# Second feed-forward products in Strassen's form, norms moved to the scalar engine, and a new order of the steps, in a two-layer graph network

## Chip, cores, metric

One core of one Trainium2 chip. The metric is the device time of one execution in microseconds (us); I quote the median of the runs of a kernel with the lowest and the highest. All runs compared here were in the fast state. Engine names are those of the profile: PE is the matrix engine (TensorE), PEld its weight loads, DVE the vector engine (VectorE), ACT the scalar engine (ScalarE), POOL GpSimd. `L338` is line 338 of the kernel whose profile is shown, so line numbers differ by kernel.

## The reference, cut to what matters

The input is `x`, 128 graphs of 128 nodes and 256 features in f32, with an adjacency matrix for each. Two layers follow. Each ends in a feed-forward network of 256 → 1024 → 256 with residual and layer norm.

```python
# layer 0: attention in 8 heads, values chosen by relation r
scores = einsum('bhid,bhjd->bhij', q, k) / sqrt(dh);  attn = softmax(scores)
out = sum over r of einsum('bhij,bhjd->bhid', attn * (adj == r), v_r)
x = ln(src + out @ Wo + bo, g1, beta1)                     # norm 0
x = ln(x + gelu(x @ W1 + b1) @ W2 + b2, g2, beta2)         # norm 1
# layer 1: two graph attentions, then
h = ln(x + gat(gat(x)), g_ln1, b_ln1)                      # norm 2
return ln(h + relu(h @ w_ff1 + b_ff1) @ w_ff2 + b_ff2)     # norm 3
```

## The kernel before

It works in 32 groups of four graphs (T = 512 rows). Every phase of a group is a Python generator, and `in_order(...)` takes steps from several generators in a list written by hand. The instructions then run in that order on each engine. In the loop the first feed-forward network (`f1`) and the graph layer (`l1`) of one group, the second network (`f2`) of another, and projections (`pr`) and attention (`at`) of a third lie between one another. The first product of each network is already in Strassen's form (7 products in place of 8); the second is plain. `seeded` is one PSUM bank into which products are added on top of a copied start.

```python
def added(S, i, p, po, res):               # residual sum into a new tile, statistics
    ...
    nc.vector.tensor_add(flat(t[:, pair(p), :]), po, flat(res[:, pair(p), :]))
    for s in range(2):
        nc.vector.bn_stats(...); nc.vector.bn_aggr(...)

def normed(S, i, bs=slice(0, G)):          # (x - mean) * rs, on VectorE
    for b in range(bs.start, bs.stop):
        nc.vector.tensor_scalar(t[:, b, :], t[:, b, :], mv[:, b, 0:1], rs[:, b : b + 1],
                                op0=ALU.subtract, op1=ALU.mult)

# in ffn(), after the first product:       # the plain second product
for p in range(G // 2):
    po = ps_1.tile([P, T], F32, tag="fe" if p else "fa", ...)
    for s in range(2):
        b = 2 * p + s
        for f in range(NF):
            nc.tensor.matmul(po[:, s * D : (s + 1) * D], hT[:, f, b * P : (b + 1) * P],
                             wb_[:, f, :], start=(f == 0), stop=(f == NF - 1))
            ...
    added(S, i, p, po, S["res", i - 1])

# the end of the program
in_order((f2, 14), (n2, 2), (n3, 4), lambda: store(S), (f2, 4))
checks()
```

Of the kernel before, what the change touches and what calls it, by code (L numbers as in the profile page):

```python
# [24 lines left out]
G = 4  # L25
# [4 lines left out]
class Weights:  # L30
# [41 lines left out]
    def constants(self):  # L72
        nc = self.nc
        self.ident = self.tile([P, P], "ident")
        make_identity(nc, self.ident)
        self.ones = self.tile([P, P // 4], "ones")
        nc.vector.memset(self.ones, 1.0)
        self.eps = self.tile([P, 1], "eps")
        nc.vector.memset(self.eps, EPS)
        self.mhalf = self.tile([P, G], "mhalf")  # L80
        nc.vector.memset(self.mhalf, -0.5)
# [22 lines left out]
def fast_pass(ctx, tc, a, out):  # L104
# [17 lines left out]
    io = ctx.enter_context(tc.tile_pool(name="io", bufs=2))  # L122
# [3 lines left out]
    small = ctx.enter_context(tc.tile_pool(name="small", bufs=4))  # L126
    dram = ctx.enter_context(tc.tile_pool(name="dram", bufs=2, space=bass.MemoryType.DRAM))
# [4 lines left out]
    def load_xT(g):  # L132
        xt = w1p.tile([P, NCH, T], F32, tag="xT", name=f"xT_{g}")
        nc.sync.dma_start(
            xt, xT[:, g * T : (g + 1) * T].rearrange("(c p) t -> p c t", p=P)
        )
        return xt
# [9 lines left out]


    k.constants()
    first = {"g": 0}  # L150
    first["xt"] = load_xT(0)
# [9 lines left out]
    first["ad"], first["xr"] = load_rest(0)  # L161
# [19 lines left out]
    FH = FF // 2  # L181
    B11, B21, B22, T4, T1, T2, T3 = range(7)

    def forms(name):

        w = k.tile([P, 7, FH], "w_" + name)
        for i, c, h in ((B11, 0, 0), (B21, 1, 0), (B22, 1, 1), (T1, 0, 1)):
            nc.sync.dma_start(
                w[:, i], a[name][c * P : (c + 1) * P, h * FH : (h + 1) * FH]
            )  # L190
        return w

    def combined(w):
        for o, p, q in ((T3, B22, T1), (T1, T1, B11), (T2, B22, T1), (T4, B21, T2)):
            nc.vector.tensor_sub(w[:, o], w[:, p], w[:, q])
# [9 lines left out]
    w2 = k.w("L0_gnn_W2")  # L205
# [3 lines left out]
    u2 = k.w("L1_gnn_w_ff2")  # L209
# [57 lines left out]
    def transposed(y, gc, bc, n):  # L267

        yT = w3p.tile([P, NCH, T], F32, tag="yT", name="yT_" + n)
# [14 lines left out]
    def added(S, i, p, po, res):  # L284

        n = f"{i}_{S['g']}"
        if p == 0:
            S["t", i] = w3p.tile([P, G, D], F32, tag="t", name="t_" + n)
            S["mv", i] = (
                c_out[:, S["g"]] if i == 3  # L290
                else small.tile([P, G, 2], F32, tag="mv", name="mv_" + n)
            )
        t, mv = S["t", i], S["mv", i]
        nc.vector.tensor_add(flat(t[:, pair(p), :]), po, flat(res[:, pair(p), :]))
        st = small.tile([P, 2, 6], F32, tag="st", name=f"st_{n}_{p}")
        for s in range(2):
            nc.vector.bn_stats(st[:, s, :], t[:, 2 * p + s, :])  # L297
            nc.vector.bn_aggr(mv[:, 2 * p + s, :], st[:, s, :])
# [8 lines left out]
    def normed(S, i, bs=slice(0, G)):  # L307

        t, mv, rs = S["t", i], S["mv", i], S["rs", i]
        for b in range(bs.start, bs.stop):  # L310
            nc.vector.tensor_scalar(  # L311
                t[:, b, :], t[:, b, :], mv[:, b, 0:1], rs[:, b : b + 1],
                op0=ALU.subtract, op1=ALU.mult,
            )
# [5 lines left out]
    def scaled(S, i, p):  # L320
        t = S["t", i]
        if p == 0:
            S["res", i] = t if i == 3 else w3p.tile(
                [P, G, D], F32, tag="res", name=f"res_{i}_{S['g']}"
            )
        o = S["res", i]
        nc.vector.tensor_mul(o[:, pair(p)], t[:, pair(p)], over(rows[i][0], 2))
        nc.vector.tensor_add(o[:, pair(p)], o[:, pair(p)], over(rows[i][1], 2))

    def norm(S, i):  # L330
# [5 lines left out]
        for p in range(G // 2):  # L336
            scaled(S, i, p)
# [4 lines left out]
    def turned(S, i):  # L342
        n = f"{i}_{S['g']}"
        S["xT", i + 1] = yT = transposed(S["t", i], *cols[i], n)
# [7 lines left out]
        nc.vector.tensor_sub(ys[:, 1], ys[:, 0], a11)  # L352
        nc.vector.tensor_sub(ys[:, 3], a12, ys[:, 1])

    def ffn(S, i, wa, ba, func, wb_):

        n = f"{i}_{S['g']}"
        yT, ys = S["xT", i], S["yS", i]
        a11, _, a12, a22 = (yT[:, c, h * TH : (h + 1) * TH] for c in range(2) for h in range(2))
        s1, s2, s3, s4 = (ys[:, m] for m in range(4))  # L360
        hT = w1p.tile([P, NF, T], F32, tag="hT", name="hT_" + n)
        RN = NF // 4

        def product(bank, form, m, r, start=False):


            for s in range(2):
                f = 2 * r + s
                nc.tensor.matmul(  # L369
                    bank[:, s * TH : (s + 1) * TH], wa[:, form, f * P : (f + 1) * P], m,  # L370
# [3 lines left out]
        def hidden(r, k2, h):  # L374

            f = k2 * NF // 2 + 2 * r
            return hT[:, f : f + 2, h * TH : (h + 1) * TH]

        def activated(src, r, k2, h):
            for s in range(2):  # L380
                f = k2 * NF // 2 + 2 * r + s
                nc.scalar.activation(  # L382
                    hidden(r, k2, h)[:, s], src[:, s * TH : (s + 1) * TH] if src is not None
                    else hidden(r, k2, h)[:, s], func, bias=ba[:, f : f + 1],
# [13 lines left out]
        for r in range(RN):  # L398
            pe = ps_1.tile([P, T], F32, tag="fe", name=f"ph7_{n}_{r}")
# [5 lines left out]
            u2 = w1p.tile([P, T], F32, tag="u2", name=f"u2_{n}_{r}")  # L405
            nc.scalar.copy(u2, seeded)
# [3 lines left out]
            yield  # L410
            product(pe, T4, a22, r)
            nc.vector.tensor_add(hidden(r, 0, 1), halves(pe), halves(u2))  # L412
            activated(None, r, 0, 1)
            yield
            product(seeded, T1, s1, r)
            nc.vector.tensor_add(hidden(r, 1, 1), halves(seeded), halves(p7))  # L416
            activated(None, r, 1, 1)
# [5 lines left out]
            activated(seeded, r, 1, 0)  # L423
            if r + 1 < RN:
                nc.scalar.copy(seeded, pa)
            yield
        for p in range(G // 2):
            po = ps_1.tile([P, T], F32, tag="fe" if p else "fa", name=f"po_{n}_{p}")
            for s in range(2):
                b = 2 * p + s  # L430
                for f in range(NF):
                    nc.tensor.matmul(  # L432
                        po[:, s * D : (s + 1) * D], hT[:, f, b * P : (b + 1) * P], wb_[:, f, :],
                        start=(f == 0), stop=(f == NF - 1),
                    )
                    if f == NF // 2 - 1 or (f == NF - 1 and s == 0):
                        yield
            added(S, i, p, po, S["res", i - 1])
            yield
# [4 lines left out]
    def second_ffn(S):  # L444
        yield from ffn(S, 3, u1, c1, AF.Relu, u2)

# [11 lines left out]
    def entered(g):  # L458

        xt = load_xT(g)  # L460
        ad, xr = load_rest(g)
        return dict(xt=xt, ad=ad, xr=xr, g=g)

    def prepared(S):
        g, xr, ad = S["g"], S["xr"], S["ad"]
# [64 lines left out]
    def sums(S, p):  # L530

        e, pm = S["e", p], S["pm", p]
# [21 lines left out]
        den = rd.rearrange("p u c i -> p (u c i)")  # L554
# [3 lines left out]
        nc.vector.tensor_reduce(c_att[:, 0, g, p : p + 1], den, AX.X, ALU.min)  # L558
        nc.vector.reciprocal(den, den)  # L559
        for u in range(2):  # L560
            bs = slice((2 * p + u) * P, (2 * p + u + 1) * P)
            nc.vector.tensor_mul(oT[:, :, bs], pav[:, u], rd[:, u])

    def attention(S):
# [3 lines left out]
        for p in range(G // 2):  # L568
# [4 lines left out]
            sums(S, p)  # L573
            yield
        for p in range(G // 2):
# [8 lines left out]
            added(S, 0, p, po, S["xr"])  # L584
            yield

    def spread(columns, n):
# [3 lines left out]
        line = small.tile([G, P], F32, tag="line", name="line_" + n)  # L591
# [7 lines left out]
    def edges(target, source, S, l):  # L599
# [3 lines left out]
        for b in range(G):  # L603
            nc.scalar.activation(  # L604
                s[:, b, :], target[:, b, :], AF.Identity, bias=source[:, b, :]
            )
        nc.vector.scalar_tensor_tensor(s, s, ALPHA, s, op0=ALU.mult, op1=ALU.max)
        yield
        nc.scalar.activation(s, s, AF.Exp)
# [12 lines left out]
    def layer1(S):  # L622
# [28 lines left out]
        for p in range(G // 2):  # L651
# [7 lines left out]
            added(S, 2, p, po, S["res", 1])  # L659
        yield  # L660

    def store(S, bs=slice(0, G)):
# [3 lines left out]
            S["t", 3][:, bs],  # L666
# [436 lines left out]
```

## Time and profile before

| | before |
|---|---|
| time, median of 4 runs | 2887.47 us (2886.09 to 2888.1) |
| TensorE / weight loads / VectorE / ScalarE busy | 98% / 76% / 70% / 45% |
| TensorE's streaming, counted | 2751.5 us |
| span less streaming ("lost") | 136.6 us |
| of it: first 60 us / between / last 108 us | 27.3 / 74.3 / 34.9 us |

Streaming is not a view of the profile. I multiply each TensorE record by the start-to-start pace of its kind in stretches without a wait, as the prediction does below (its sum with rounded paces is 2749; the full count gives 2751.5). The rest of the span is "lost": waits, and time at a lower clock. It is needed because the busy share hides waits of a few hundred ns, as the modelled ends reach over them. The same counting is used for all kernels below.

One more view of before is wanted for later: the timeline of TensorE in its last 90 us, four of the lines with a wait. The columns are start, length, engine, line, operation, count; in brackets the idle time ahead and what ended it.

```profile
2820.79 3.81 PE L643 MATMUL py<-wh,gs 128*128 128x258 f32 x8 [3.86 <-DVE gs L619]
2836.68 1.99 PE L655 MATMUL pg<-yh,gs 128*128 128x256 f32 x8 [0.83 <-DVE gs L619]
2843.88 2.30 PE L273 MATMUL pt<-ident,t 128*128 128x128 f32 x8 [3.48 <-DVE t L311]
2881.21 0.19 PE L769 MATMUL pflag<-ones,good 128*1 128x1 f32 x2 [4.84 <-DVE good L767]
```

Near the end no other group is left to fill in, so each hand-over to VectorE is open. After the wait of 3.86 us eight matmuls took 3.81 us, twice their usual time: the clock had been lowered.

### The profile page before, as it was taken

How to read it: one execution, taken by the hardware profiler on the slowest of the kernel's cores; microseconds unless marked ns; L12 is line 12 of the kernel's file. 1: busy time of each engine (PE TensorE's matmuls, PEld its weight loads, DVE VectorE, ACT ScalarE, POOL GpSimd, SP SyncE). 2: the span in 40 equal slices, each digit the busy share in tenths (PEclk: the TensorE clock that was granted, in tenths of full speed). 3: DMA queues.
4: the chain of work that ended last, by engine and by line, in shares of the span. 5: the costliest groups of instructions: out<-in, count | busy, mean ns of one | idle time of the engine just before them, and what ended most of it. 6: DMA issues, size and time to landing. Idle time of an engine off the chain costs nothing.

```text
span 2888.1 us, 44301 instructions
## 1 busy us (share of the span) xinstructions
PE 2839.6 (98%) x17744; PEld 2206.1 (76%) x17744; DVE 2015.8 (70%) x4595; ACT 1312.5 (45%) x2759; POOL 141.5 (5%) x137
## 2 busy tenths in 40 slices
PE   7999999999999999999999999999999999999997
PEld 4677777777787777787777777777877777877775
DVE  6577666777667777667776677776677776677764
ACT  3435445445455345454454454453553444544542
POOL 0000000000000000000000000000000000000000
PEclk9999999999999999999999999999999999999998
DMA  5000111010111000110001110101110001101000
GB/s 152 23 27 12 34 34 34 23 34 12 34 34 34 23 26 20 34 34 26 30 12 34 34 34 23 34 12 34 34 33 24 20 26 34 34 26 30 12 19 20
DMA packets 68469, 86.82 MB, mean 30 GB/s; under 512 B 8096, under 2 KB 46368, under 8 KB 68256
## 3 DMA queue, kind: packets, MB, share of 16 engines
q1 hardware_dynamic: 67424, 83.52, 9.2%
q8 instruction: 141, 2.31, 0.3%
q14 instruction: 72, 0.59, 0.1%
q10 hardware_dynamic: 832, 0.40, 0.0%
HBM read 66.99 MB, written 16.91 MB: 29 GB/s over the span
## 4 chain that ended last, share of the span: by engine, by line
PE 95%; DVE 2%; ACT 1%; DMA 1%; SPq 0%; issue 0%; POOL 0%; ACTq 0%; DVEq 0%; POOLq 0%
PE po L432 30%; PE ph L369 15%; PE seeded L369 12%; PE pq L483 7%; PE pv L493 7%; PE pw L630 4%; PE pwo L580 4%; PE pav L546 4%; PE pt L273 3%; PE ps L511 2%; PE pden L537 2%; PE py L643 2%; PE pg L655 2%; ACT hT L382 0%; DVE rd L559 0%; DVE st L297 0%
## 5 line engine op out<-in xcount | busy, mean ns | idle before, releaser
L432 PE MATMUL po<-w_L_gnn_W,hT 128*128 128x256 f32 x2048 | 480.7, 383 | 0.0
L432 PE MATMUL po<-w_L_gnn_w_ff,hT 128*128 128x256 f32 x2048 | 463.3, 380 | 0.0
L432 PEld LDWEIGHTS po<-w_L_gnn_W,hT 128*128 128x128 f32 x2048 | 384.8, 190 | 87.5 <-issue 37.0
L432 PEld LDWEIGHTS po<-w_L_gnn_w_ff,hT 128*128 128x128 f32 x2048 | 385.1, 190 | 54.2
L305 POOL TENSOR_TENSOR rs<-rs,mhalf 128x4 f32<-128x4 f32 x129 | 138.9, 1076 | 2702.5 <-DVE rs L304 2702.5
L517 ACT ACTIVATE e<-ps 128x512 f32<-128x512 f32 x256 | 132.3, 603 | 295.8 <-PE ps L511 295.8
L493 PE MATMUL pv<-wv,xT 128*128 128x512 f32 x512 | 240.7, 593 | 2.0 <-ACT e L517 2.0
L297 DVE BATCH_NORM_STATS2 st<-t 128x6 f32<-128x256 f32 x512 | 210.4, 411 | 8.8
L559 DVE RECIPROCAL rd<-rd 128x512 f32<-128x512 f32 x64 | 214.6, 3353 | 2.2
L412 DVE TENSOR_TENSOR hT<-ph,u 128x512 f32<-128x512 f32 x128 | 88.1, 688 | 178.7 <-ACT hT L382 128.6
L369 PE MATMUL seeded<-yS,w_L_gnn_w_ff 128*128 128x256 f32 x768 | 204.3, 388 | 4.2 <-DVE hT L416 2.8
L369 PE MATMUL seeded<-yS,w_L_gnn_W 128*128 128x256 f32 x768 | 199.7, 382 | 1.5 <-DVE hT L416 0.8
L311 DVE TENSOR_SCALAR t<-t,mv,rs 128x256 f32<-128x256 f32 x384 | 132.5, 408 | 92.5 <-POOL rs L305 92.5
L369 PEld LDWEIGHTS seeded<-yS,w_L_gnn_W 128*128 128x128 f32 x768 | 143.1, 190 | 66.6 <-issue 37.1
L369 PE MATMUL ph<-yT,w_L_gnn_W 128*128 128x256 f32 x768 | 193.1, 381 | 0.4 <-ACT yT L276 0.4
L369 PE MATMUL ph<-yT,w_L_gnn_w_ff 128*128 128x256 f32 x768 | 191.1, 385 | 0.0
L396 ACT COPY seeded<-ph 128x512 f32<-128x512 f32 x64 | 36.5, 570 | 302.4 <-PE ph L369 302.4
L369 PEld LDWEIGHTS ph<-yT,w_L_gnn_w_ff 128*128 128x128 f32 x768 | 143.6, 191 | 34.9 <-issue 14.1
L369 PEld LDWEIGHTS seeded<-yS,w_L_gnn_w_ff 128*128 128x128 f32 x768 | 138.2, 190 | 37.8 <-DVE hT L416 13.9
L525 DVE TENSOR_TENSOR pm<-e,adj 128x512 f32<-128x512 f32 x256 | 159.9, 686 | 6.8 <-ACT e L517 6.8
L369 PEld LDWEIGHTS ph<-yT,w_L_gnn_W 128*128 128x128 f32 x768 | 143.8, 191 | 23.4 <-ACT yT L276 1.1
L604 ACT ACTIVATE gs<-spread,wh 128x128 f32<-128x128 f32 x128 | 40.9, 390 | 242.4 <-DMA spread<-hbm 242.4
(131 smaller groups left out, 4611.0 us busy)
## 6 DMA issues: line engine op xcount, KB each, us to landing
xT<-in_xT_dram SPq DMA_DIRECT2D x32, 512.0 KB, 4.0
x<-in_x_dram SPq DMA_DIRECT2D x32, 512.0 KB, 5.1
spread<-hbm SPq DMA_DIRECT2D x64, 256.0 KB, 4.3
out_dram<-t SPq DMA_DIRECT2D x31, 512.0 KB, 2.9
adj<-in_adjT_dram SPq DMA_DIRECT2D x32, 256.0 KB, 6.0
w_L_gnn_W<-in_L_gnn_W_dram SPq DMA_DIRECT2D x4, 256.0 KB
w_L_gnn_W<-in_L_gnn_W_dram SPq DMA_DIRECT2D x1, 1024.0 KB
w_L_gnn_w_ff<-in_L_gnn_w_ff_dram SPq DMA_DIRECT2D x4, 256.0 KB, 6.3
```

What stands on the lines that cost most here:

```text
L297: nc.vector.bn_stats(st[:, s, :], t[:, 2 * p + s, :])
L305: nc.gpsimd.tensor_tensor(rs[:, bs], rs[:, bs], k.mhalf[:, bs], op=ALU.pow)
L311: nc.vector.tensor_scalar(t[:, b, :], t[:, b, :], mv[:, b, 0:1], rs[:, b : b + 1], op0=ALU.subtract, op1=ALU.mult,)
L369: nc.tensor.matmul(bank[:, s * TH : (s + 1) * TH], wa[:, form, f * P : (f + 1) * P], m, start=start and s == 0, stop=True, skip_group_chec ...
L432: nc.tensor.matmul(po[:, s * D : (s + 1) * D], hT[:, f, b * P : (b + 1) * P], wb_[:, f, :], start=(f == 0), stop=(f == NF - 1),)
L483: nc.tensor.matmul(pq, w[:, c, m * P : (m + 1) * P], xt[:, c, :], start=(c == 0), stop=(c == NCH - 1),)
L493: nc.tensor.matmul(pv, xt[:, c, b * P : (b + 1) * P], wv[:, c].rearrange("p r d -> p (r d)"), start=(c == 0), stop=(c == NCH - 1),)
L517: nc.scalar.activation(e[:, s], pss[s], AF.Exp, scale=SCALE)
L525: nc.vector.tensor_mul(pm[:, s], S["e", p][:, s], S["ad"][:, pair(p), None, :].to_broadcast([P, 2, NCH, P]),)
L546: nc.tensor.matmul(pav[s * DH : (s + 1) * DH, u, c, :], v[:, d0 : d0 + DH], m[:, s, u, c, :], start=(r == 0), stop=(r == 1),)
L559: nc.vector.reciprocal(den, den)
L580: nc.tensor.matmul(po[:, s * D : (s + 1) * D], oT[:, c, b * P : (b + 1) * P], wo[:, c, :], start=(c == 0), stop=(c == NCH - 1),)
```

## The change

Its intent: spend the slack of the weight loads and of the other engines to cut TensorE's streaming.

1. The second products take Strassen's form too: 7 products of 128 columns, with sums on VectorE before them (`h2`, `h3`) and in their eviction.
2. The residual is kept in place in one tile `x`; the normalisation of norms 0, 1 and 2 goes to ScalarE. The weight combinations go to GpSimd, the minimum of the denominators to a Relu on ScalarE.
3. The order is new everywhere: group 1's projections lie within group 0's attention, the two networks overlap by a step, and two steps (`gelu`, `exp`) load ScalarE's function tables ahead of need.

The diff, cut to its core:

```diff
-        for p in range(G // 2):                       # plain second product (shown above)
-            ...
+        pa = ps_1.tile([P, T], F32, tag="fa", name=f"po1_{n}")
+        product2(pa, B11, hidden(0, 0), True)
+        nc.scalar.copy(seeded[:, : 2 * P], pa[:, : 2 * P])
+        yield
+        pe = ps_1.tile([P, T], F32, tag="fe", name=f"po7_{n}")
+        product2(pe, T3, h3, True)
+        nc.vector.tensor_add(x22, bank(pe), quarter(1, 1))
+        yield
+        product2(seeded, T2, h2)
+        nc.vector.tensor_add(x21, bank(seeded), quarter(1, 0))
+        ...                                           # four more: B21, T1, T4, B22
 def normed(S, i, bs=slice(0, G)):
+        if i < 3:
+            nc.vector.scalar_tensor_tensor(sh, mv[:, :, 0], -1.0, rs, op0=ALU.mult, op1=ALU.mult)
         for b in range(bs.start, bs.stop):
-            nc.vector.tensor_scalar(t[:, b, :], t[:, b, :], mv[:, b, 0:1], rs[:, b : b + 1], ...)
+            if i < 3:
+                nc.scalar.activation(x[:, b, :], x[:, b, :], AF.Identity,
+                                     bias=sh[:, b : b + 1], scale=rs[:, b : b + 1])
+            else:
+                nc.vector.tensor_scalar(x[:, b, :], x[:, b, :], mv[:, b, 0:1], rs[:, b : b + 1], ...)
# the loop's order (one of its lists)
-                    n3, (f1, 2), pr, (f1, 2), l1, (n0_, 2), (f1, 2), l1, f1, n3, (f1, 2), pr, n3,
+                    pr, lambda: turned(S1, 0), pr, f1, f2_, n3, f1, n0_, (f1, 4), n0_, (f1, 2), n3, l1, f1, f1, l1, n3,
# the end
-        in_order((f2, 14), (n2, 2), (n3, 4), lambda: store(S), (f2, 4))
+        in_order((f2, 14), (n2, 2), (n3, 4), lambda: store(S), (f2, 2))
         checks()
-        for p in range(G // 2):
+        in_order((f2, 4))
+        for p in (1, 0):
```

## The prediction

> **What bounds the kernel now.** I read the page's busy shares first, then the chain of work that ended last, the groups of instructions, and last the timeline of TensorE, to get the pace of one instruction of each kind.
>
> ```profile
> span 2888.1 us, 44301 instructions
> PE 2839.6 (98%) x17744; PEld 2206.1 (76%) x17744; DVE 2015.8 (70%) x4595; ACT 1312.5 (45%) x2759; POOL 141.5 (5%) x137
> ...
> PE 95%; DVE 2%; ACT 1%; DMA 1%; SPq 0%; issue 0%; POOL 0%; ACTq 0%; DVEq 0%; POOLq 0%
> ```
>
> TensorE is busy 98% and is 95% of the chain, so the time is what TensorE has to stream plus the places where it waits. The part that the change cuts is the costliest group, the second feed-forward products, with their weight loads:
>
> ```profile
> L432 PE MATMUL po<-w_L_gnn_W,hT 128*128 128x256 f32 x2048 | 480.7, 383 | 0.0
> L432 PE MATMUL po<-w_L_gnn_w_ff,hT 128*128 128x256 f32 x2048 | 463.3, 380 | 0.0
> L432 PEld LDWEIGHTS po<-w_L_gnn_W,hT 128*128 128x128 f32 x2048 | 384.8, 190 | 87.5 <-issue 37.0
> ...
> L511 PE MATMUL ps<-qT,kT 32*128 32x128 f32 x2048 | 77.0, 283 | 2.3 <-DVE t L294 1.3 <-DVE v L497 0.9
> ```
>
> There are 4096 records, though the program has 32 groups x 2 networks x 32 = 2048 such products: each f32 matmul of the program is two matmuls and two weight loads on the engine. Means (383 ns) and busy sums are of overlapping, modelled spans, so I use starts instead. The timeline of TensorE, columns start, length, what, how many:
>
> ```profile
> 1519.40 5.34 PE L432 MATMUL po<-w_L_gnn_w_ff,hT 128*128 128x256 f32 x24
> 1524.58 1.04 PE L273 MATMUL pt<-ident,t 128*128 128x128 f32 x8
> ...
> 1494.16 1.17 PE L511 MATMUL ps<-qT,kT 32*128 32x128 f32 x32
> ...
> 1495.27 0.30 PEld L369 LDWEIGHTS ph<-yT,w_L_gnn_w_ff 128*128 128x128 f32 x2
> ```
>
> From 1519.40 to 1524.58 are 24 matmuls of 256 columns: 5.18/24 = **216 ns each**. The last line is two weight loads of 128 columns lying 0.30 us from first start to last end; one takes 189 ns, so they start **108 ns** apart: a load has some 80 ns of latency and 108 ns of occupation. The scores (third line) are the nearest thing to the new products that this kernel holds: 128-column f32 weights with 128 moving columns, four row groups side by side. Their eight quartets take 1.17 us; less the last one's 0.27, the 20 ns within a quartet and 0.10 us in which the first waits for its own load, seven steps remain in 0.78 us: **112 ns a step**, where streaming alone would take 108.
>
> Multiplying all counts by such paces (216 ns for 256 columns, 429.5 for 512, 218 to 219 for 258 and 260, 109 for transposes, 110 to 112 for a quartet of 128 columns, 430 for one of 512): 4096 x 216 = 885; the first products 3584 x 216 = 774; projections 1024 x 429.5 = 440; the 258s and 260s 168; the other 256s 166; transposes 84; attention 113 + 57 + 55; 7 for the rest. Sum **2749 us of streaming**; the other **139 us** are waits. By windows: the first 60 us hold 33 us of streaming (27 lost), the last 108 us hold 73 (35 lost), and the stretch between loses about 77, of which 49 in 300 to 2600:
>
> ```profile
> 0.00:60.00 60.00, 45.41 (x295) 26.42 (x296) 39.26 (x83) 14.23 (x26) 3.69 (x9) 0.91 0.65 182
> 300.00:2600.00 2300.00, 2300.00 (x14483) 1796.93 (x14483) 1634.46 (x3723) 1071.72 (x2259) 113.97 (x105) 1.00 0.09 28
> ```
>
> (Columns: stretch, length, busy PE, PEld, DVE, ACT, POOL, clock, DMA.) In the long middle the busy share is 100% though 2% of it is waits: the modelled ends hide gaps. The clock is full.
>
> **What the Trainium skill says.** "TensorE: Matmul & The Clock Gate", section "LDWEIGHTS (loading the stationary operand)": a load takes columns / 1.2 GHz, whatever the rows; 107 ns for 128. The trace agrees (108 between starts). Same page, "Back-to-back issue gap": in a stream of load and matmul pairs both set the spacing; it measures 81 ns for 128 bf16 columns where the matmul alone would need 56. That is a warning for this change, which makes the moving side as short as the load; no full-height f32 pair of that shape is in this trace, only the scores' 112. "Perfetto Trace Analysis", section "Identifying the Most-Contended Engine": judge by load busy share, not matmul busy share; at 76% here it leaves room, and it is what the change spends. "VectorE: DVE Perf Modes", section "The TRN2 errata": an f32 tensor_tensor takes (N+151)/0.96 ns, 691 for 512 and 424 for 256; the groups here show 684 to 692 and 417 to 425.
>
> **The change, part by part.**
>
> *Second products.* Per network and group 32 program matmuls of 256 columns become 7 products x 2 x 4 = 56 of 128 columns. In engine instructions: 4096 x 216 = 885 us become 7168 x 112 = 803 us. Gain **82 us**, all on TensorE, the path. Only 7/8 of the columns, 12.5%, could be saved; the pace of 112 rather than 108 takes a quarter of that back. At 109 ns it would be 104 us.
>
> *Vector work added:* per network and group (64 times) three sums per round for two rounds, 6 x 0.69, two more of 512 columns on the hidden values, 2 x 0.69, and six evictions of 256 columns at about 0.40 in place of two of 0.68. That is 5.52 + 2.4 - 1.36 = 6.6 us, 420 us in all. *Removed:* the normalisation of three of the four norms goes to ScalarE (384 x 0.345 = 132 us), the minimum of the denominators too (64 x 0.69 = 44), the weight combinations go to GpSimd (6); 96 tiny products come in (15). Sum 2016 + 420 - 132 - 44 - 6 + 15 = **2270 us**, 81% of the new span.
>
> *ScalarE:* 384 normalisations of 256 columns at about 0.53 (the 256-column activation at 0.44 and a scale operand more) = 203, the Relu that replaces the minimum with its accumulator read 64 x 0.9 = 57, 64 copies at 0.37 = 24, the table preloads' dummies 12: 1312 + 296 = about **1610 us**, 57%. The table loads (64 or so) stay as many; their place is now chosen. Neither engine becomes the bound by its sum; both lie beside TensorE.
>
> *Residual in place, deeper input buffers:* this frees memory for four buffers of x and the 7 forms of the second weights; no time by itself.
>
> *Beginning:* the first 60 us show TensorE waiting 4.05 us for oT and 3.83 us for the first norm, where VectorE had just been held 3.3 us by the weight combination. That goes to GpSimd, and eight projection steps of group 1 (about 14 us of streaming that had to be done anyway) lie in these holes. I give it 8 of the 27 us. The 256-column reciprocals (half of 3.35 us) let others in between. The tail keeps its chain of statistics, root, scale, store and flag: 35 us again.
>
> *Sum:* streaming 2749 - 82 = 2667; beginning 19; end 35; the middle 77, plus 7 because VectorE, now at 81%, answers later. Total **2805 us**, 2.9% below 2888.
>
> **Rivals.**
> 1. *Load-bound pairs.* Full-height pairs run slower than the scores' 112. For it: the skill's 81 against 56, and no slack at all between load and stream. Against: back-to-back loads at 108, scores at 112 with the same number of columns. At 121 the gain is 18 us and the time about 2870; at 123 it is nothing. I give 10% to 118 or more.
> 2. *Waits take its place.* The last sums of the first product (h3, h2) feed weight loads of the second, through VectorE, ScalarE and VectorE again: 0.69 + 1.0 + 0.69 and hand-overs, about 3 us, against 0.86 + 1.8 us of TensorE work of the same network if nothing lies between. The new order puts a step of another generator there nearly everywhere, as the listing of instructions per engine shows. If half of the 64 still lost 1 us, 32 us: about 2837, within 2%.
> 3. *A much better order.* If the middle's 77 us fell by half, 2765. The old order was already tuned, and VectorE has 250 us more to do, so I give this little.
>
> **Range and chances.** The gain of 82 has a spread of 15 or so from the pace; the waits one of 25. So 8 in 10: 2772 to 2845. The line of 2% is 2830. Chance of faster 0.80, same 0.17, slower 0.03.
>
> **What would show it.** The second products: 7168 records, steps of 16 taking 1.79 us; if the pace is 120, rival 1. VectorE near 2270 us, ScalarE near 1610. Slices of TensorE still 9, with the first at 8; if the waits of the new products for h2, h3 or the copies into the seeded bank sum to over 30 us, rival 2. I am wrong altogether if the pace is right and the span is not below 2845, or if it is below 2772.

## The result, and the profile after

The changed kernel is correct and takes **2838.78 us** (2836.74 to 2840.0, 4 runs) against 2887.47; the ratio is 0.9831, with a 95% interval of 0.9814 to 0.9848. A ratio here is the mean time of one kernel's fast runs over the mean of the other's fast runs of the same rounds, so not quite the ratio of the medians. The gain is 1.7%: inside the predicted range, but the prediction gave "within 2%" a chance of only 0.17 and put its centre at 2805.

The page of the changed kernel: span, busy times, and the engines' shares in the chain that ended last.

```profile
span 2837.9 us, 51798 instructions
...
PE 2776.8 (98%) x20816; PEld 2233.8 (79%) x20816; DVE 2176.8 (77%) x5068; ACT 1568.5 (55%) x3395; POOL 162.2 (6%) x153
...
PE 86%; ACT 7%; DVE 2%; issue 0%; POOL 0%; POOLq 0%; DVEq 0%; ACTq 0%
```

TensorE is still busy 98%, but it makes up 86% of the chain, not 95%; ScalarE has 7%, where it had 1%. This points to something on ScalarE that holds TensorE up, though it is busy only 55% of the time. The groups of instructions (line, engine, operation, shape, count | busy us, mean ns | idle time ahead of them):

```profile
L338 ACT ACTIVATE x<-x,sh,rs 128x256 f32<-128x256 f32 x384 | 199.4, 597 | 180.5 <-DVE sh L333 180.5
...
L409 PE MATMUL po<-w_L_gnn_W,hT 128*128 128x128 f32 x1536 | 190.1, 277 | 0.0
...
L409 PEld LDWEIGHTS po<-w_L_gnn_W,hT 128*128 128x128 f32 x1536 | 181.7, 192 | 5.7 <-issue 0.5
```

The first line is the normalisation on ScalarE. It cost 199 us of ScalarE's time, near the 203 that I had put down. New is its last column: ScalarE stood idle 180.5 us in front of these instructions, waiting for VectorE's `sh`. That alone doesn't say that time was lost. In the loop this idle time stands before one norm of each group, norm 0 (4.67 us at 1577.79, for example), and its transposes on TensorE follow there without a wait (1581.13). The Trainium skill, "ScalarE: Activation LUTs", section "What ACT_TABLE_LOAD costs", gives an activation 186 ns + 0.833 ns a column, 93 more for each operand that is a column of values, and an overlap of 93 between neighbours. For 256 columns and two such operands that is an estimated 585 ns, 492 from start to start; the trace agrees with 597 and, in the queue shown below, four in 2.07 us.

The pace of the new products is seen in the timeline of TensorE in the last network, and what befell it there too:

```profile
2806.36 1.95 PE L409 MATMUL po<-w_L_gnn_w_ff,h 128*128 128x128 f32 x16
2808.15 1.95 PE L409 MATMUL seeded<-w_L_gnn_w_ff,h 128*128 128x128 f32 x16
2809.93 1.95 PE L409 MATMUL po<-w_L_gnn_w_ff,hT 128*128 128x128 f32 x16
2816.74 3.62 PE L409 MATMUL seeded<-w_L_gnn_w_ff,hT 128*128 128x128 f32 x16 [4.85 <-DVE x L496]
2820.19 1.95 PE L409 MATMUL po<-w_L_gnn_w_ff,hT 128*128 128x128 f32 x16
```

Sixteen records in 1.79 us (2806.36 to 2808.15), **112 ns each**, as predicted; all 7168 are there. The fourth line waited 4.85 us, and its sixteen then took 3.45 us (2816.74 to 2820.19), 216 ns each.

Counted as before, in the prediction's own windows:

| us | before | predicted | after |
|---|---|---|---|
| streaming | 2751.5 | 2667 | 2669.6 |
| lost in the first 60 us | 27.3 | 19 | 20.3 |
| lost between | 74.3 | 84 | 100.8 |
| lost in the last 108 us | 34.9 | 35 | 47.2 |
| span | 2888.1 | 2805 | 2837.9 |

Streaming and the beginning came as predicted. Of the 33 us that are missing, 17 are in the long stretch between and 12 at the end.

**Between.** The loop's steady part repeats every 85.73 us (one group; 29 periods counted), before 87.746. Where the new loss sits shows when the TensorE starts are compared with the pace, over 300 to 2600 us. The products into `seeded` in the second network lost 18.0 us there (8.1 before), and the transposes of norm 2 (`pt`) 5.7, where I found none over 90 ns before: 15.6 us together. (Some 9 of the 26.5 us that this stretch lost more lie before 300 us or after 2600, and I did not follow them up.) The products on `h2` and `h3`, which my second rival had named, show only the steps of some 100 ns that follow the scores' blocks in both kernels. The timeline of ScalarE in one period:

```profile
1543.99 0.59 ACT L445 COPY p<-ph 128x512 f32<-128x512 f32 x1 [2.01 <-PE ph L400]
1544.48 2.07 ACT L338 ACTIVATE x<-x,sh,rs 128x256 f32<-128x256 f32 x4
1546.45 0.56 ACT L449 COPY p<-seeded 128x512 f32<-128x512 f32 x1
1546.92 2.05 ACT L594 ACTIVATE e<-ps 128x512 f32<-128x512 f32 x4
```

and of TensorE beside it:

```profile
1543.80 1.03 PE L400 MATMUL seeded<-yS,w_L_gnn_w_ff 128*128 128x256 f32 x4
1544.75 1.17 PE L588 MATMUL ps<-qT,kT 32*128 32x128 f32 x32
1545.86 1.13 PE L400 MATMUL ph<-yT,w_L_gnn_w_ff 128*128 128x256 f32 x4
1547.07 1.13 PE L400 MATMUL seeded<-yS,w_L_gnn_w_ff 128*128 128x256 f32 x4
```

The `seeded` product of 1543.80 was finished by 1544.7, and the copy of it (L449) is needed before the next product into that bank. But norm 1's four activations stand ahead of the copy in ScalarE's queue, so it starts at 1546.45, and the product at 1547.07 comes 0.25 us late. Here ScalarE was not idle in front of the norm: the 2.07 us of the norm's own work delayed the copy.

**The end.** The timeline of VectorE while TensorE waited 4.85 us:

```profile
2811.02 1.38 DVE L343 TENSOR_SCALAR x<-x,c_out,rs 128x256 f32<-128x256 f32 x4 [1.19 <-POOL rs L325]
2812.32 1.29 DVE L356 TENSOR_TENSOR x<-x,r_L_gnn_g_ln 128x512 f32<-128x512 f32 x2
2813.52 1.29 DVE L356 TENSOR_TENSOR x<-x,r_L_gnn_b_ln 128x512 f32<-128x512 f32 x2
2814.73 0.42 DVE L492 TENSOR_TENSOR x<-po,x 128x256 f32<-128x256 f32 x1
2815.06 0.73 DVE L764 TENSOR_REDUCE ext<-c_gat 128x1 f32<-128x256 f32 x2
...
2816.26 0.42 DVE L496 TENSOR_TENSOR x<-seeded,x 128x256 f32<-128x256 f32 x1
```

The eviction L496, for which `seeded` waits, takes 0.42 us. It stood behind the last norm of the previous group and behind the range checks, neither of which anyone needed yet. A plain second product has no such eviction in the middle; Strassen's form has, and the written order at the end took no account of it. The other open waits of the end (TensorE, to be compared with the four lines of before):

```profile
2760.50 3.81 PE L726 MATMUL py<-wh,gs 128*128 128x258 f32 x8 [4.25 <-DVE gs L702]
2778.82 3.55 PE L738 MATMUL pg<-yh,gs 128*128 128x256 f32 x8 [3.08 <-DVE gs L702]
2786.37 2.80 PE L290 MATMUL pt<-ident,x 128*128 128x128 f32 x8 [4.00 <-ACT x L338]
...
2831.14 0.19 PE L858 MATMUL pflag<-ones,good 128*1 128x1 f32 x2 [7.22 <-DVE good L856]
```

Every wait is longer, and the clock falls more often: six times in the last 108 us, three times before. The granted clock over the sixteen matmuls after the 4.85 us (windows view: stretch, length, busy PE, PEld, DVE, ACT, POOL, clock, DMA):

```profile
2816.90:2820.10 3.20, 3.20 (x16) 3.20 (x17) 0.17 (x2) 0.00 (x0) 0.00 (x0) 0.51 0.13 44
```

The Trainium skill, "TensorE: Matmul & The Clock Gate", section "What's actually happening", has the array at half rate after an idle window of about 3.4 us and back at full rate after a busy one. The trace agrees in kind: clock 0.51 and 216 ns in place of 112 after the 4.85 us. In all the clock was low for 54.3 us of the changed kernel and 36.8 of before; half of the difference, some 9 us, is the most that is lost by it (worked out, and contained in the "lost" above; where TensorE waits anyway, a low clock costs nothing).

### The profile page after: what moved, and what is told of

Same layout as the page of the kernel before. It is cut to its first block, busy times and chain, and to the rows that moved or that the text cites. A ratio compares the mean times of both kernels' runs of the same rounds, so it can differ in the third digit from the quotient of the medians.

```text
span 2837.9 us, 51798 instructions
## 1 busy us (share of the span) xinstructions
PE 2776.8 (98%) x20816; PEld 2233.8 (79%) x20816; DVE 2176.8 (77%) x5068; ACT 1568.5 (55%) x3395; POOL 162.2 (6%) x153
## 4 chain that ended last, share of the span: by engine, by line
PE 86%; ACT 7%; DVE 2%; issue 0%; POOL 0%; POOLq 0%; DVEq 0%; ACTq 0%
PE ph L400 14%; PE po L409 14%; PE seeded L409 12%; PE seeded L400 11%; PE pq L560 7%; PE pv L570 6%; PE pw L713 4%; PE pav L624 4%; ACT x L338 4%; PE pwo L662 4%; PE pt L290 3%; PE pden L615 2%; PE py L726 2%; PE pg L738 2%; ACT e L594 1%; PE ps L588 1%
## 5 line engine op out<-in xcount | busy, mean ns | idle before, releaser
L338 ACT ACTIVATE x<-x,sh,rs 128x256 f32<-128x256 f32 x384 | 199.4, 597 | 180.5 <-DVE sh L333 180.5
L455 DVE TENSOR_TENSOR hT<-seeded,p 128x512 f32<-128x512 f32 x128 | 88.5, 692 | 148.3 <-PE seeded L400 148.3
L400 PE MATMUL ph<-yT,w_L_gnn_w_ff 128*128 128x256 f32 x768 | 199.0, 388 | 0.0
L310 DVE BATCH_NORM_STATS2 st<-x 128x6 f32<-128x256 f32 x512 | 192.5, 418 | 7.7
L409 PE MATMUL po<-w_L_gnn_W,hT 128*128 128x128 f32 x1536 | 190.1, 277 | 0.0
L409 PE MATMUL po<-w_L_gnn_w_ff,hT 128*128 128x128 f32 x1536 | 187.0, 275 | 0.0
L409 PEld LDWEIGHTS po<-w_L_gnn_w_ff,hT 128*128 128x128 f32 x1536 | 184.0, 192 | 3.2
L409 PEld LDWEIGHTS po<-w_L_gnn_W,hT 128*128 128x128 f32 x1536 | 181.7, 192 | 5.7 <-issue 0.5
L400 PEld LDWEIGHTS seeded<-yS,w_L_gnn_W 128*128 128x128 f32 x768 | 138.4, 190 | 52.7 <-issue 15.6
L602 DVE TENSOR_TENSOR pm<-e,adj 128x512 f32<-128x512 f32 x256 | 161.7, 693 | 4.1 <-ACT e L594 4.1
L424 ACT ACTIVATE hT<-hT,c_L_gnn_b 128x256 f32<-128x256 f32 x256 | 109.4, 497 | 61.4 <-DVE hT L455 60.3
L570 PEld LDWEIGHTS pv<-wv,xT 128*128 128x128 f32 x512 | 90.7, 192 | 66.1 <-issue 63.6
```

The costliest lines, as they stand in the source:

```text
L310: nc.vector.bn_stats(st[:, b % 2, :], S["x"][:, b, :])
L338: nc.scalar.activation(x[:, b, :], x[:, b, :], AF.Identity, bias=sh[:, b : b + 1], scale=rs[:, b : b + 1],)
L400: nc.tensor.matmul(bank[:, s * TH : (s + 1) * TH], wa[:, form, 0, f * P : (f + 1) * P], m, start=start and s == 0, stop=True, skip_group_c ...
L409: nc.tensor.matmul(bank[:, s * P : (s + 1) * P], m[:, f, s * P : (s + 1) * P], wb_[:, form, f, :], start=start and s + f == 0, stop=True, ...
L570: nc.tensor.matmul(pv, xt[:, c, b * P : (b + 1) * P], wv[:, c].rearrange("p r d -> p (r d)"), start=(c == 0), stop=(c == NCH - 1),)
L602: nc.vector.tensor_mul(pm[:, s], S["e", p][:, s], S["ad"][:, pair(p), None, :].to_broadcast([P, 2, NCH, P]),)
```

## The experiments

There were two questions: what the wait is that took the place of the gain, and which part of the change brought it. Theory A, mine after the result: the norms on ScalarE and the queues' order at the end cost some 30 us; the Strassen form and the new order are sound. Rival B: the form itself brings the waits (VectorE answers later, or its sums are too late), whoever applies the norms. All twelve kernels are correct.

### e1: the norms back on VectorE

```diff
-        if i < 3:            # both places in normed()
+        if False:
```

> The changed kernel with the three norms back on VectorE, nothing else. After the change TensorE streams 2670 us as predicted but loses 168 us to waits, 32 more than before (136.6). Theory A: the norms on ScalarE cost it, since a block takes 491 ns there against 322 on VectorE, the transposes wait for each block at the ends, and in the steady periods they wait 0.21 us for ScalarE. Then 6 to 13 us less than the changed kernel (2838.8): 2826 to 2833, and the 491 ns steps are gone. Theory B: VectorE is the scarce engine in the new form, and the norms had to leave it. Then 5 to 25 us more: 2844 to 2864, with the steady period above 85.73 us.

Measured: 2844.1 us (2843.59 to 2845.09), ratio 0.9853. So ScalarE's norms are worth 5 us *in this order*; taking them away is no cure. The period went from 85.73 to 86.10. Both are what theory B had forecast (2844 to 2864, a longer period), not mine. VectorE in one period:

```profile
1530.65 1.28 DVE L506 TENSOR_TENSOR hT<-hT,h 128x512 f32<-128x512 f32 x2
1531.85 1.38 DVE L343 TENSOR_SCALAR x<-x,mv,rs 128x256 f32<-128x256 f32 x4
1533.14 2.49 DVE L602 TENSOR_TENSOR pm<-e,adj 128x512 f32<-128x512 f32 x4
1535.55 0.42 DVE L509 TENSOR_TENSOR x<-po,x 128x256 f32<-128x256 f32 x1
...
1536.89 0.66 DVE L574 TENSOR_TENSOR v<-pv,r_L_gnn_bv 128x512 f32<-128x512 f32 x1
```

and the wait that it makes on TensorE:

```profile
1535.05 1.88 PE L570 MATMUL pv<-wv,xT 128*128 128x512 f32 x4
1537.60 1.07 PE L615 MATMUL pden<-e,ones 128*32 128x512 f32 x8 [0.67 <-DVE v L574]
```

Norm 2 (L343) pushes the masking (L602) and the eviction of `v` back, and `pden` waits. These waits come to 24.9 us over 300 to 2600, while the waits of `pt` and of `seeded` on ScalarE's norms are gone. One wait was exchanged for another.

### e5: ScalarE for norm 2 alone

```diff
-        if i < 3:
+        on_act = i == 2 and S["g"] < NG - 1
+        if on_act:
```

> The changed kernel with only the norm of the graph layer (number 2) on ScalarE, and of the last group not even that; the other norms on VectorE. In e1 the steady period was 86.10 us against 85.73, by one new wait of 0.83 us for a value eviction that stood behind norm 2 on VectorE; in the changed kernel ScalarE's norm 1 delays a copy by 0.25 us, and the ends lose some 3 us each at 491 ns steps. If a norm's cost is its place in one engine's queue and not the engine's sum: period 85.4 to 85.6, ends shorter by 6 in sum, so 2822 to 2831. If VectorE's sum matters (2240 us or so): no better than 2838.

Measured: 2824.21 us (2820.24 to 2827.41), ratio 0.9779; period 85.304. The `pden` wait stays away, and the loss on the `seeded` products falls from 18.0 to 8.4 us, its size before. The steady part lost 57.4 us where the change lost 69.8. So norms 0 and 1 cost 14.6 us more in ScalarE's queue than on VectorE (2838.8 less 2824.2), 12.4 of them in the loop. The time lies where I had forecast it for the place in the queue, but not for the reason at the ends: the trace is 12.3 us shorter than that of the change (2825.6 against 2837.9), all of it in the loop, while I had put down 6 us for the ends.

### e2 and e4: plain second products in the new order

e2 puts the plain second products of before (with the sum into the one tile `x`) into the changed kernel; e4 puts the norms back on VectorE as well.

```diff
-        pa = ps_1.tile(...)                  # the seven products
-        ...
+        for p in range(G // 2):              # plain, as before
+            ...
+            added(S, i, p, po)
```

> The changed kernel with the second products in the plain form (4096 engine matmuls of 256 columns, no h2 and h3 sums, plain weights); norms on ScalarE, in-place tile and new order kept. Streaming returns to about 2751 us. If the Strassen form's own dependencies make the 32 us of extra waits, the waits fall back to about 137: 2885 to 2893. If norms on ScalarE and the new order make them, they stay near 168: 2915 to 2925. In the first case the Strassen form is worth about 50 us on its own, in the second about 80.

> Both undone: plain second products and norms on VectorE, in-place tile and new order kept. With e1, e2 and the changed kernel this is a square of four. If the norms' place costs the same in both forms, this differs from e2 as e1 does from the changed kernel (theory A: some 6 to 13 us less than e2). If the norms had to leave VectorE only because of the Strassen form, this one is faster than e2 or equal while e1 is slower than the changed kernel. What the new order alone brings is this run against the kernel before: the start lost 20 us in place of 27, so 2880 to 2886 if nothing else differs.

Measured: e2 2946.46 us (2945.23 to 2948.0), ratio 1.0206; e4 2922.69 us (2921.22 to 2924.33), ratio 1.0123. Both expected ranges were missed by 20 us and more. One branch written for e4 came true: it is faster than e2, while e1 is slower than the change, as if the norms had to leave VectorE for the Strassen form's sake. The old order (e9, below) shows that this holds in the new order only. With plain products the new order is itself 35 us slower than the kernel before; over 300 to 2600 us of e4, 27.3 us go to the first-network product `ph<-yS`, which waits for the eviction of the bank that the second network still holds. One of these waits on TensorE:

```profile
1550.40 1.13 PE L398 MATMUL ph<-yS,w_L_gnn_W 128*128 128x256 f32 x4 [0.78 <-DVE x L317]
```

The new order lets the two networks overlap at their ends, which seems to suit seven products and not eight (my reading; why is not shown). From this I took the new order to be what the Strassen form needs. The next pair was to show it.

### e7 and e8: the old order

e7 is the changed kernel with the lists of the kernel before (at the beginning and in the loop; `merged` joins the steps into which the change cut the attention and the graph layer). e8 has, besides, the plain second products and VectorE's norms: it is the kernel before with the small parts of the change (tile in place, GpSimd's combinations, the Relu, the reciprocal in two halves).

```diff
-                    pr, lambda: turned(S1, 0), pr, f1, f2_, n3, f1, n0_, (f1, 4), n0_, ...
+                    n3, (f1, 2), pr, (f1, 2), l1, (n0_, 2), (f1, 2), l1, f1, n3, (f1, 2), ...
```

> The changed kernel (Strassen second products, norms on ScalarE, one tile in place) in the order of the kernel before: its interleaving of the steps word for word, group 1's projections within the first network again, no explicit table loads; the last network's order as changed. If the new order is what makes room for the Strassen form (its eviction chains and the split reciprocals need steps of other work between), this is much slower: 2870 to 2910, the Strassen form then gains little or nothing in the old order. If the order is worth only the start, 2842 to 2850.

> Plain second products, norms on VectorE, old order: what is left of the change is the tile in place, ScalarE's minimum, the split reciprocal and GpSimd's weight combinations. If these are neutral, as the prediction has it, this is the kernel before within 5 us: 2882 to 2892. With e4 (2922.7), e7 and the changed kernel it makes a square of form and order: if it is near 2887, the new order costs the plain form about 35 us.

Measured: e8 2889.94 us (2888.55 to 2890.61), ratio 1.0013: the small parts are neutral within 4 us, as expected. e7 2917.48 us (2915.22 to 2918.42), ratio 1.0104, above even the upper expectation. That seemed to confirm that form and order belong together. But e7 also has the norms on ScalarE, and its group line is striking:

```profile
L338 ACT ACTIVATE x<-x,sh,rs 128x256 f32<-128x256 f32 x384 | 199.3, 590 | 641.5 <-DVE sh L333 641.5
```

The busy time is that of the changed kernel, but ScalarE stood idle **641.5 us** in front of its norms. What lies behind them in the queue (ScalarE, then TensorE):

```profile
1572.79 2.08 ACT L338 ACTIVATE x<-x,sh,rs 128x256 f32<-128x256 f32 x4 [9.57 <-DVE sh L333]
1574.78 2.02 ACT L602 ACTIVATE e<-ps 128x512 f32<-128x512 f32 x4
```

```profile
1570.95 1.17 PE L596 MATMUL ps<-qT,kT 32*128 32x128 f32 x32
1572.06 2.05 PE L409 MATMUL po<-w_L_gnn_W,hT 128*128 128x128 f32 x16
1575.40 1.99 PE L578 MATMUL pv<-wv,xT 128*128 128x512 f32 x4 [1.29 <-ACT e L602]
```

The scores were ready at about 1572.1, and ScalarE had been idle for 9 us; yet the exponentials began at 1574.78, because norm 2 stood ahead of them and waited for VectorE. `pv` needs a bank that the exponentials free, and waited 1.29 us. So the pair e7 and e8 had changed two things at once, and e9 was needed.

### e9 and e10: the old order with other places for the norms

```diff
 # e9: e7 with
-        if i < 3:
+        if False:
 # e10: e7 with
-        if i < 3:
+        on_act = i == 2 and S["g"] < NG - 1
+        if on_act:
```

> The Strassen form in the old order (e7: 2917, period of a pair of groups 88.21 us) with the three norms put back on VectorE. Theory A (e7 was slow because ScalarE's norm applications stood in its queue ahead of the exponentials and of the copies that the seeded products wait for: 1.46 + 0.81 us of a period): at least 2 us of each period come back, 2842 to 2865. Theory B (the old order itself does not suit the Strassen form: its sums on VectorE come too late for the second half of the products, whoever applies the norms): the waits move to VectorE and the time stays at 2890 to 2925.

> The same with ScalarE applying norm 2 alone, and not in the last group (the placement that gained 0.43 us a period in the new order, e5). Under theory A of e9 it lies near e9, within 15 us and above 2840. Under theory B it lies within 15 us of e7 (2917) too. If it lies clearly under 2838 the new order was not needed at all and my reading of the square of form and order is wrong.

("A pair of groups" in this text is a slip of mine: the period is that of one group.)

Measured: e9 **2822.5 us** (2821.52 to 2825.15), ratio 0.9781. This falls below both expectations. Its direction is theory A's: 3.0 us of each period came back, from 88.209 to 85.193. For e10 I had written that a time clearly under 2838 in the old order would mean that the new order was not needed. It is e9 that met this: *the new order was not needed*, and my reading of form and order was wrong. e10: 2869.7 us (2869.07 to 2870.89), ratio 0.9943, near neither e9 nor e7, so neither theory's forecast for it held. Norm 2 alone on ScalarE, which gained 20 us in the new order (e1 to e5), costs 47 us in the old one: over 300 to 2600 us the waits of `pv` come to 47.5 us, as in e7 (45.9); in e9 to 5.6. ScalarE's idle time in front of norm 2 tells the two orders apart. In e10 it is the line below; in e5 the same 124 instructions have 10.5 us.

```profile
L339 ACT ACTIVATE x<-x,sh,rs 128x256 f32<-128x256 f32 x124 | 64.3, 589 | 288.8 <-DVE sh L334 288.8
```

The same place as in e7, in the profile of e9 (its page; then ScalarE and TensorE):

```profile
span 2820.2 us, 51612 instructions
...
PE 2759.4 (98%) x20816; PEld 2243.7 (80%) x20816; DVE 2282.4 (81%) x5356; ACT 1369.8 (49%) x2951; POOL 162.1 (6%) x153
...
PE 94%; DVE 3%; ACT 1%; SPq 1%; DMA 1%; issue 0%; POOL 0%; ACTq 0%; POOLq 0%; DVEq 0%
```

```profile
1524.59 2.06 ACT L602 ACTIVATE e<-ps 128x512 f32<-128x512 f32 x4 [8.92 <-PE ps L596]
```

```profile
1523.40 1.17 PE L596 MATMUL ps<-qT,kT 32*128 32x128 f32 x32
1524.51 2.05 PE L409 MATMUL po<-w_L_gnn_W,hT 128*128 128x128 f32 x16
1526.40 1.88 PE L578 MATMUL pv<-wv,xT 128*128 128x512 f32 x4
```

ScalarE was idle here too, but it waited for the scores themselves and began at once; `pv` follows without a wait. VectorE is at 81%, with more to do than in the change, and the chain is 94% TensorE again. So VectorE's share alone was not the trouble.

All nine combinations of form, order and place of the norms that ran, with the loss in the 29 steady periods (some 2,500 us):

| second products | order | norms 0 to 2 on | median, us | period, us | lost in 29 periods, us |
|---|---|---|---|---|---|
| plain | old | VectorE (e8) | 2889.9 | 87.955 | 60.1 |
| plain | new | VectorE (e4) | 2922.7 | 89.184 | 95.7 |
| plain | new | ScalarE (e2) | 2946.5 | 89.749 | 112.1 |
| Strassen | old | VectorE (e9) | 2822.5 | 85.193 | 54.2 |
| Strassen | old | norm 2 ScalarE (e10) | 2869.7 | 86.739 | 99.0 |
| Strassen | old | ScalarE (e7) | 2917.5 | 88.209 | 141.7 |
| Strassen | new | VectorE (e1) | 2844.1 | 86.099 | 80.5 |
| Strassen | new | norm 2 ScalarE (e5) | 2824.2 | 85.304 | 57.4 |
| Strassen | new | ScalarE (the change) | 2838.8 | 85.730 | 69.8 |

Read it in pairs. From e8 to e9 the Strassen form, with the order of the end that goes with it, gives 67 us, and its 54.2 us of loss in the loop are those of the kernel before (54.0). So rival B falls for the loop. From e9 to the change, the new order and ScalarE's norms *together* take 16 us back; each alone does worse, unless only norm 2 moves. (Both keep the small parts.)

### e3 and e6: the end

e3 is the changed kernel with the checks and the last norm of the previous group drawn forward, between the products of the last network. e6 is e5 with that, and with the last graph layer's steps spread between the products before it.

```diff
-        in_order((f2, 14), (n2, 2), (n3, 4), lambda: store(S), (f2, 2))
-        checks()
-        in_order((f2, 4))
+        in_order(
+            (f2, 2), checks, f2, n3, (f2, 2), n3, (f2, 2), n2, f2, n2, (f2, 2), n3, f2, n3,
+            lambda: store(S), (f2, 9),
+        )
```

> The changed kernel with only the last group's order changed: the last norms' work of the two last groups and the range checks go to VectorE early in the last network instead of between its second products, where the eviction of the second Strassen product stood behind them and TensorE waited 5.0 us, followed by 3.6 us at half clock. If that queueing is the cause, 5 to 9 us less than the changed kernel: 2830 to 2834, and the 5.0 us wait is gone. If the tail is bound by VectorE's sum and not by its order, the wait only moves: within 2 us of 2838.8.

> e5 with e3's order for the last network and the last group's edge steps drawn forward by some steps of the product beside them. If the three causes are separate they add: e5 less 5 (e3) less 2 to 4 for the edge steps: 2814 to 2824. If the tail is one chain that only shifts, it is within 3 us of e5 less 5.

Measured: e3 2833.46 us (2830.68 to 2834.68), ratio 0.9813, 5 us below the change; e6 **2815.36 us** (2810.72 to 2820.14), ratio 0.9758, the fastest of all. Both as expected. The fast runs of e6 fall into two pairs: 2810.7 and 2811.4 us at a granted clock of 0.994, 2819.3 and 2820.1 at 0.990; those of e5 differ likewise (2820.2 and 2821.7 at 0.993 and 0.992, 2826.7 and 2827.4 at 0.990). Pair against pair, e6 gains 7 to 10 us. Its trace is of a run of the quicker pair. TensorE's waits of over 2 us that are left at the end of e6:

```profile
2738.89 2.01 PE L727 MATMUL py<-wh,gs 128*128 128x258 f32 x8 [2.61 <-DVE gs L703]
2756.59 2.83 PE L739 MATMUL pg<-yh,gs 128*128 128x256 f32 x8 [3.08 <-DVE gs L703]
2763.02 2.29 PE L290 MATMUL pt<-ident,x 128*128 128x128 f32 x8 [3.59 <-DVE x L344]
...
2802.21 0.19 PE L861 MATMUL pflag<-ones,good 128*1 128x1 f32 x2 [7.22 <-DVE good L859]
```

The wait of 4.85 us for an eviction is gone. That for `py` fell from 4.25 to 2.61, after which its eight matmuls ran in 2.01 us, no longer in 3.81. That full clock is partly luck: in e12, which has the same end, the same wait of 2.61 us was followed by a fall of the clock, and the eight took 2.47 us. The last stretch, from the start of the last graph layer on, lost 32.3 us where the change lost 43.1 there, and the clock was low for 36.3 us in all, as before the change (36.8); in the trace of e12 it was low for 46.2.

### e11: without the table preloads

```diff
-                    (f1, 3), pr, n3, lambda: store(st[g - 1]), f1, f1, exp, l1, l1, pr, f1, l1, f1,
+                    (f1, 3), pr, n3, lambda: store(st[g - 1]), f1, f1, l1, l1, pr, f1, l1, f1,
-                n0, l1, gelu, f2, l1, f2,
+                n0, l1, f2, l1, f2,
```

> The changed kernel without the two explicit table preloads of each group in the loop; the loads then come at the first instruction that needs the other table, as many as before (some 60 in the loop, 1283 ns each). If their chosen place hides them: each load now stands ahead of a wanted exponential or Gelu, up to 1.3 us at 60 places, 2850 to 2900. If ScalarE has room at these places anyway: 2836 to 2843, same.

Measured: 2847.91 us (2847.1 to 2848.6), ratio 0.9866: 9 us slower than the change, between the two expectations. The loads stay 67 in number. Without the preload a new wait appears, `ph<-yT` in the first network on the Gelu ahead of it, 11.4 us over 300 to 2600 us. So the preloads together do gain, and the wait that appears is where Gelu begins; each preload apart was not tested. Of the new order, this is a part that works.

### e12: fuller beginning

```diff
-            at, (pr1, 2), (at, 2), at, pr1, at, pr1, (n0, 2), lambda: turned(first, 0), (n0, 2),
+            at, (pr1, 2), (at, 2), at, pr1, at, pr1, (n0, 2), (pr1, 2), lambda: turned(first, 0), (n0, 2),
```

> e6 (2815) with the last two projection steps of group 1 before the first transpose of group 0, where TensorE waits for the first norm at the start. If that wait is open (3 us or so): 2811 to 2815. If the projections only pushed later work back: 2815 to 2819. Anything outside of this would be unexplained.

Measured: 2817.04 us median of six runs, of which five were fast (2812.06 to 2818.78; one slow run of 3178 us at a clock of 0.846 is left out of the ratio; the median of the five is 2816.21), ratio 0.9752 with an interval of 0.9739 to 0.9765. That cannot be told from e6 (0.9742 to 0.9775). The trace says why: the first 60 us lost 17.7 us and not 20.9, and the 62 us that follow 14.1 and not 10.9. The filled hole only moved.

## Why the prediction was right or wrong

**The second products: right.** Pace 112 ns, 7168 records, streaming down by 81.9 us (predicted 82). Rival 1, a pace bound by the loads, is refuted. With e8 and e9 the form, with its own order of the end, is seen in the time: 67 us. The other 14 or 15 of the 82 go to waits, 13 of them in the stretch from the last graph layer to the end (41.4 us lost there in e9, 28.6 in e8). How much of these 13 is the form and how much its order of the end was not separated.

**The beginning: right in size, in half of its reason.** Predicted 27 to 19, measured 27.3 to 20.3. Of the two reasons that I gave, the projections drawn into the holes hold and GpSimd's combinations do not: e9, which has these but the old order, loses 27.3.

**The long stretch: wrong, and this is the step that failed.** I wrote "plus 7 because VectorE, now at 81%, answers later", and let the normalisation go to ScalarE as pure removal, because "neither engine becomes the bound by its sum; both lie beside TensorE". The stretch lost 26.5 us more, not 7 more than my count gave it. e9 has VectorE at 81% and lost 79.5 us there: 5 more than before, near the 7 predicted (whatever made them). What cost was the part for which I had put down nothing: where norms on ScalarE stand in a queue that runs in the written order. In the new order norm 1's own work delays a copy that TensorE waits for; norms 0 and 1 together cost 14.6 us by e5. In the old order a norm that waits for VectorE holds up exponentials that are ready, though ScalarE is idle (641.5 us in front of the norms in e7, 288.8 in e10); it costs 95 us by e7 and 47 by e10, each against e9. Idle time in front of a norm is not itself a cost: of the 180.5 us of the change, I found none in the loop that TensorE waited for. I had read the order only as places where another generator fills in, which is TensorE's side of it.

**The end: wrong in size.** Predicted "35 again", measured 47.2. "The tail keeps its chain" overlooked that Strassen's form evicts in the middle, behind the last norms and the checks on VectorE, and that the clock falls about such a wait, as it does for 3.4 us or more in all seven traces with this wait of 4.85 us. e9, with the norms on VectorE, has the same: 43.8. e3 and e6 show that it is a matter of the order.

**The busy sums** were near enough and told nothing of the waits: ScalarE predicted 1610, measured 1568; VectorE 2270 and 2177.

**Rival 2, "Waits take its place",** had the size, by luck, 2837 against 2838.8 measured, but not the place. The sums `h2` and `h3` cost nothing that I can find, and the waits were on the norms and on the end's evictions. I had given this too little weight: with the streaming right, everything hung on the waits, and a spread of 25 us about a mean of plus 0 left out that moving work to another engine makes a new queue, not just a new sum.

**What stays open.** e9 with the end of e6 did not run. By the losses of the last stretch (41.4 and 32.3 us) it would take about 2822.5 - 9.1 = 2813 us, an estimate that assumes that the parts add up (this study shows how little that may be assumed), and that takes the 32.3 from one of e6's two quicker runs. Nor is it shown which single move in the new order's loop brings `pden` and norm 2 into conflict in e1.

## What to carry to other kernels

Moving work to an engine with idle time is free only if nothing wanted stands behind it in that engine's queue: look at what is next in line behind the moved instruction, whether it is ready, and who waits for it; the busy share doesn't show this, and idle time ahead of the instruction is only a hint. Norm 2 on ScalarE gained 20 us in one order and cost 47 in another, so a change of engine and a change of order must be tried in all combinations; one that changes both at once can hide that half of it is not needed. And when the middle of a kernel is tight, look at its end apart: here a wait there was paid in full, and often again in clock.

## What the Trainium skill lacked or had wrong

- "TensorE: Matmul & The Clock Gate", "Back-to-back issue gap", has no figure for f32: it gives 81 ns measured for 128 columns where the matmul alone needs 56, without naming the type (the prediction takes it for bf16). For f32 pairs of a full-height weight load and 128 moving columns the trace shows 112 ns, against 108 between bare loads: there is almost no such surcharge, and the ratio does not carry over.
- The same page, "What's actually happening", puts the fall to half rate after an idle window of about 3.4 us and says that the window is free-running, not set by the kernel. Here shorter waits are followed by the fall in one trace and not in another. After a wait of 2.02 us the second group of four matmuls (256 columns) took 1.10 us in e6 (at 2684.04) and 2.04 us in e12 (at 2686.78); after the wait of 2.61 us, e6 kept the full clock and e12 did not. In the changed kernel a wait of 3.08 us (at 2778.82) was followed by eight matmuls in 3.55 us, which take 1.89 at full rate. No length of wait that is safe comes out of these traces.
- "Perfetto Trace Analysis", "Identifying the Most-Contended Engine", takes occupancy as a fair measure for the vector and scalar engines. It did not tell these kernels apart: e7 and e9 differ by 95 us with ScalarE at 53% and 49%. What did was the idle time ahead of one group, 641.5 us, with ready exponentials behind it; I found no page that says how to find such an engine in a profile, idle while ready work stands behind a waiting instruction.
